# The place of two late steps, one on ScalarE and one on VectorE, in a kernel bound by TensorE

## The chip, the core and the metric

The kernel runs on one core of a Trainium2 chip. The metric is the device time of one execution in microseconds (us), as the median of several. The engines that matter are TensorE (PE in the profile; its weight loads are listed as PEld), VectorE (DVE), ScalarE (ACT) and SyncE (SP), which issues nearly all transfers. Each engine takes its instructions in the order in which the program lists them. They wait for one another through semaphores.

## What is computed

Eight batches of 256 tokens with 1024 features. Each batch goes through its own 1024 x 1024 matrix, chosen by an index. What comes out goes through one common 1024 x 1024 layer with a bias, and through a mixture of eight low-rank experts (rank 16) that a softmax router weighs. The input is added at the end.

```python
def cond(x, weight, adapter_ids):                  # per batch: y = x W[id]^T
    return jnp.einsum('bsi,boi->bso', x, weight[adapter_ids])

def ffn(x, base_W, base_b, router_W, router_b, A, B, expert_map):
    base_out = jnp.einsum('btd,od->bto', x, base_W) + base_b
    probs = jax.nn.softmax(jnp.einsum('btd,nd->btn', x, router_W) + router_b, axis=-1)   # 15 logits
    topk_p, topk_i = jax.lax.top_k(probs, E)                                             # E = 8
    onehot = (expert_map[topk_i][..., None] == jnp.arange(E)).astype(x.dtype)
    w = jnp.einsum('btk,btke->bte', topk_p, onehot)
    h = jnp.einsum('btd,erd->bter', x, A)                                                # R = 16
    return base_out + jnp.einsum('bter,eor->bto', h * w[..., None], B) * 2.0

out = x + ffn(cond(x, weight, ids), ...)
```

All of it is float32.

## The kernel before

The kernel has two stages. In both, PE, VectorE, ScalarE and SyncE take their instructions in the order in which the Python code writes them (`manual_schedule`), so a line that moves in the code moves in the queue of its engine.

**First stage, one batch after the other (the loop over b at L435).** The product of a batch with its matrix is done in the Strassen-Winograd manner: both sides are cut in four quadrants, and seven products of quadrants replace eight. Each of them is a `block` (L287): four float32 matmuls of 128 x 512, which the trace lists as eight. Three PSUM accumulators, pa, pb and pc, with two buffers each, collect the blocks. In batches 2 to 6 the blocks come in this order, with the quadrant sums S1 to S4 of the weights and T1 to T4 of x:

1. a11 b11 into pa; ScalarE copies pa to m0[:, 0] (L458).
2. a12 b21 into pb (`first_results`, L461); VectorE adds m0[:, 0] and transposes in squares of 32 (`flip`).
3. S1 T1 into pc; ScalarE copies pc to m1[:, 1] (L488).
4. S2 T2 added to pa; ScalarE copies pa to m0[:, 1] (L490).
5. S4 b22 added to pc (`by_s4`, L468); VectorE adds m0[:, 1] (L470) and transposes; then ScalarE moves all of m0, the first half of the result, to its place in y with sixteen copies of 32 partitions (`moves`, L308).
6. S3 b12 added to pa (`by_s3`, L474); VectorE adds m1[:, 1] (L476) and transposes.
7. `project` of the batch before (L129): PE multiplies y by the experts' A and the router's matrix together (143 columns, into ph, L136).
8. a22 T4 added to pa, which VectorE transposes into m1[:, 0].

The sixteen moves of the second half, m1, are left in `behind` for the next batch: four before the copy L458, twelve after it. VectorE works out the sums of the next batch's weights (L405 to L417) between its additions, and prepares the common layer's weights for the second stage (L325).

`project` also returns the steps of the routing: `logits` (with exp and the copy of h on ScalarE, L155 and L156), `softmax`, `top`, two `route_to` and `weigh` (L193), which multiplies h by the weights of the experts and transposes the product in squares of 32. After it stands a `turn` (L250): sixteen ScalarE copies of 32 x 64 elements (L255) that put the squares where they belong in hwT. In batches 2 to 7 the turn of the projection made one batch earlier is issued in `first_results`. In batches 2 to 6 that is after item 2. Batch 7 calls `first_results` later, after L490. Batch 0 and batch 1 have no turn to issue.

**Second stage, two groups of four batches (L679).** The common layer is multiplied in the Strassen-Winograd manner twice over. The outer seven products (the loop at L756) are each a `product` (L597) of seven inner blocks, now with 128 x 256 matmuls. Four of the seven outer products also add the experts' part (L588), from hwT. Between the inner blocks stand `gap(0)` to `gap(6)`. A gap runs the steps listed for it in `gaps`, which mostly append VectorE work to the queue `soon`; then `fill(2)` issues two entries of `soon`. After the last block the rest of `soon` is issued. The differences that the next product needs (L229) go to the head of `soon`, in gaps 0, 3 and 4.

The first outer product (n = 0, `here == 0`) also makes the first terms of the outer product with `first_terms`: for each of the four quarters (i, j) a pair of subtractions, y then t (L732). Quarters (0,0) and (0,1) enter in gap 1, (1,0) in gap 4, (1,1) in gap 6. Batch 6 was projected at the end of the first stage and only its `logits` were issued there; `steps_of` holds its five remaining routing steps, and they enter `soon` in gap 2 of this product. Its turn is issued after the next product, and batch 7 is projected there. ScalarE copies the first blocks of a product out of PSUM with the bias in the first outer product (L618); in the next ones VectorE does it, with an addition (L609).

Of the kernel before, what the change touches and what calls it, by code (L numbers as in the profile page):

```python
# [28 lines left out]
def kernel(  # L29
# [216 lines left out]
    def run(steps, n=None):  # L246
        for _ in range(len(steps) if n is None else min(n, len(steps))):
            steps.popleft()()

    def turn(b, hw):  # L250

        to = hwTs[b // GB][:, b % GB // 2, b % 2].rearrange("p (j a t) -> p j a t", j=NTT, a=4)
        return deque(
            (
                lambda a=a, r=r: nc.scalar.copy(  # L255
                    to[32 * r : 32 * r + 32, :, a, :],
                    hw[32 * a : 32 * a + 32, :, ts(r, 32)],
                )
            )
            for r in range(4)  # L260
            for a in range(4)
        )


    with ExitStack() as phase:
# [167 lines left out]
        waiting = None  # L433
        behind = deque()
        for b in range(B):  # L435
            last = b == B - 1

            b11, b12, b21, b22 = x[:, 0, 0], x[:, 1, 0], x[:, 0, 1], x[:, 1, 1]
            if not last:
                x, nq = load(b + 1)  # L440
            if b > 0:
                if not last:
                    third_sum(q)
                deque(prepare(b - 1))
                if last:
                    third_sum(q)
            prepare_load(b)
            if b == 1:
                nc.sync.dma_start(up[:, :2].rearrange("p h q o -> p (h q o)"), bT)

            pa = ps.tile([P, OH], F32, name="pa")
            pb = ps.tile([P, OH], F32, name="pb")
            pc = ps.tile([P, OH], F32, name="pc")

            m0, m1 = ms[:, 0], ms[:, 1]
            block(pa, q["a11"], b11, True)
            run(behind, 4)
            nc.scalar.copy(m0[:, 0], pa)  # L458
            run(behind)

            def first_results():  # L461
                block(pb, q["a12"], b21, True)
                nc.vector.tensor_add(m0[:, 0], pb, m0[:, 0])
                flip(m0[:, 0], m0[:, 0])
                if waiting:
                    run(turn(*waiting))

            def by_s4():  # L468
                block(pc, q["s4"], b22, False)
                nc.vector.tensor_add(m0[:, 1], pc, m0[:, 1])  # L470
                flip(m0[:, 1], m0[:, 1])
                run(moves(b, 0, m0))

            def by_s3():  # L474
                block(pa, q["a21"], b12, False)
                nc.vector.tensor_add(m1[:, 1], pa, m1[:, 1])  # L476
                flip(m1[:, 1], m1[:, 1])

            if not last:
                first_results()  # L480
            if b == 0:
                pd = ps.tile([P, OH], F32, name="pb")
                block(pd, q["a22"], t4, True)
                nc.scalar.copy(m1[:, 0], pd)
            if not last:
                nt1, nt2, nt4 = turns(x)
            block(pc, q["s1"], t1, True)
            nc.scalar.copy(m1[:, 1], pc)  # L488
            block(pa, q["s2"], t2, False)
            nc.scalar.copy(m0[:, 1], pa)  # L490
            if b == 0:
                by_s4()
                by_s3()
                nc.vector.tensor_add(m1[:, 0], pa, m1[:, 0])
                flip(m1[:, 0], m1[:, 0])
                first_sum(nq)
                second_sum(nq)
                fourth_sum(nq)
            elif not last:
                first_sum(nq)  # L500
                by_s4()
                if b == 1:

                    by_s3()
                    second_sum(nq)
                else:
                    second_sum(nq)
                    by_s3()
                fourth_sum(nq)
                ph = ps_h.tile([P, NTT, ER + N], F32, name="ph")  # L510
                steps, waiting = project(b - 1, ph)
                for step in steps[:3]:
                    step()
                block(pa, q["a22"], t4, False)
                flip(m1[:, 0], pa)
                for step in steps[3:]:
                    step()
            else:
                left[0] = load_left(lefts[0])
                terms = [step() for step in differences(yv[0][:, 0, 0])]  # L520
                first_results()
                by_s3()
                halves = prepare(b)
                next(halves)
                by_s4()
                deque(halves)
                block(pa, q["a22"], t4, False)
                flip(m1[:, 0], pa)
                left[1] = load_left(lefts[1])
                ph = ps_h.tile([P, NTT, ER + N], F32, name="ph")  # L530
                steps, waiting = project(b - 1, ph)
                steps.pop(0)()
            behind = moves(b, 1, m1)
            if not last:
                q, t1, t2, t4 = nq, nt1, nt2, nt4
            if b == 0:
                constants()
            if b == 1:
                nc.vector.tensor_sub(up[:, 2], up[:, 0], up[:, 1])
                nc.vector.tensor_sub(upd, up[:, :, 0], up[:, :, 1])  # L540
# [4 lines left out]
    with ExitStack() as phase:  # L545
# [21 lines left out]
        soon, later = deque(), deque()  # L567
        steps_of = steps
# [110 lines left out]
        for g in range(B // GB):  # L679
# [76 lines left out]
            for n, (right, base, into, done, *up_hw) in enumerate(seven):  # L756
                here = g * len(seven) + n
                gaps = {k: [] for k in range(7)}

                if n + 1 < len(seven):  # L760
                    follows = seven[n + 1][0]
                else:
                    follows = None if end else yv[g + 1][:, 0, 0]
                steps = [] if follows is None else differences(follows)
                nexts = []


                def advance(n, steps=steps, nexts=nexts):
                    def run():
                        soon.extendleft(  # L770
                            (lambda s=s: nexts.append(s())) for s in reversed(steps[n])
                        )

                    return run


                steps = [steps[:2], steps[2:3], steps[3:]]
                for k, m in ((0, 0), (3, 1), (4, 2)):
                    gaps[k].append(advance(m, steps))
                if here == 0:  # L780
                    gaps[2].append(lambda: soon.extend(steps_of))
                if n == 0:
                    gaps[1].append(lambda: first_terms((0, 0), (0, 1)))
                    gaps[4].append(lambda: first_terms((1, 0)))
                    gaps[6].append(lambda: first_terms((1, 1)))
                elif n in outer:
                    gaps[1].append(lambda n=n: soon.extend(outer[n]))
                if n in result_of:
                    for k, ij in enumerate([(0, 0), (1, 1), (0, 1), (1, 0)]):
                        gaps[k].append(lambda r=result_of[n] + ij: load_x(*r))  # L790
                if end and n == 6:

                    r = (1, 0, 1, 0)
                    gaps[5].append(
                        lambda: soon.append(lambda: add(u[:, 1, 0], u[:, 1, 0], xs[r]))
                    )
                if here == 0:
                    for k, count in enumerate((0, 1, 1, 4, 4, 4, 2)):
                        gaps[k].append(lambda count=count: run(behind, count))
                if here + 2 < len(lefts):  # L800

                    def fetch(m=here + 2):
                        left[m] = load_left(lefts[m])

                    gaps[5].append(fetch)
                product(
                    left.pop(here), terms, right, base, into, done, gaps, *up_hw,
                    *([None] * (2 - len(up_hw))), end and n == 6
                )
                terms = nexts  # L810
                if here == 1:
                    run(turn(*waiting))

                    ph = ps_e.tile([P, 2, S], F32, name="pe")
                    steps, waiting = project(B - 1, ph)
                    soon.extend(steps)
                elif here == 2:
                    run(turn(*waiting))
# [65 lines left out]
```

## Time and profile before

| | |
|---|---|
| median of 3 runs | 437.54 us (437.45 to 437.89) |
| the profiled execution | 437.13 us |
| its span, first to last instruction | 435.3 us |
| PE matmuls | 428.2 us busy (98%) |
| VectorE | 328.7 us (75%) |
| ScalarE | 166.7 us (38%) |
| sixteen copies of a turn (L255), 128 in all | 31.1 us, 243 ns each |
| moves (L308), 256 in all | 103.0 us, 402 ns each |
| granted TensorE clock, mean | 1.000 |
| first stage | up to 230.53 us |
| batches 3 to 6 | 28.32 us each |

The times in the trace count from the start of the span. The span is shorter than the time of the execution by 1.8 us, and the latter is what the median compares with. A line number in a row is that of the code that recorded the instruction, so blocks of the first stage all carry L290 and transposes L244; accumulators and tiles tell them apart. A matmul's end is modelled: rows of PE overlap a little, and the distance between starts says more than the durations.

### The profile page before, as it was taken

The page shows a single profiled execution, that of the slowest core. Times are in us where ns is not written, and L with a number is a line of the kernel's source. Part 1 is how long each engine was busy: PE and PEld are TensorE (multiplying, and loading weights), DVE is VectorE, ACT ScalarE, POOL GpSimd, SP SyncE. Part 2 cuts the span into 40 slices and gives each one's busy share as a digit, 9 for nine tenths or more (in the row PEclk, how much of TensorE's full clock was granted, in tenths as well). Part 3 has the DMA queues.
Part 4 walks back from the last instruction along what each step waited for, and adds up shares of the span by engine and source line. Part 5 has one row for each costly group of instructions (what it writes and reads, how often), then busy time and mean ns, then how long its engine had stood idle before and what let it go on. Part 6 is the DMA issues. An engine that isn't in the chain of part 4 may idle for free.

```text
span 435.3 us, 4931 instructions
## 1 busy us (share of the span) xinstructions
PE 428.2 (98%) x1642; PEld 293.3 (67%) x1642; DVE 328.7 (75%) x556; ACT 166.7 (38%) x458; POOL 0.7 (0%) x6
## 2 busy tenths in 40 slices
PE   8999998999999999999999999999999999999997
PEld 6344553644645446446459898888888888888886
DVE  0799999785887898988976866955597858745595
ACT  1029288665785676756928700300200200000200
POOL 0000000000000000000000000000000000000000
PEclk9999999999999999999999999999999999999999
DMA  7997987859587598791659555432968725912843
GB/s 276 416 347 256 369 332 287 304 174 353 177 302 273 223 318 304 270 333 78 209 230 372 226 179 234 159 132 78 373 227 275 274 77 201 392 62 63 300 152 139
DMA packets 32779, 106.05 MB, mean 244 GB/s; under 512 B 3058, under 2 KB 6898, under 8 KB 29554
## 3 DMA queue, kind: packets, MB, share of 16 engines
q1 hardware_dynamic: 32610, 105.21, 66.5%
q10 hardware_dynamic: 144, 0.52, 0.3%
q8 instruction: 13, 0.21, 0.2%
q14 instruction: 12, 0.10, 0.1%
HBM read 84.49 MB, written 21.23 MB: 243 GB/s over the span
## 4 chain that ended last, share of the span: by engine, by line
PE 70%; ACT 13%; DMA 7%; DVE 6%; SPq 2%; issue 2%; ACTq 0%; DVEq 0%
PE pa L579 20%; PE pa L290 14%; PE pc L579 10%; ACT y L308 7%; PE pc L290 6%; PE ph L136 5%; PE pb L579 5%; ACT hwT L255 4%; PE pc L588 3%; DMA wt<-in_wq_dram 2%; DMA late<-in_xr_dram 2%; DMA late<-in_ar_dram 2%; PE pb L588 2%; PE pa L588 1%; DVE wt L405 1%
## 5 line engine op out<-in xcount | busy, mean ns | idle before, releaser
L308 ACT COPY y<-late 32x256 f32<-32x256 f32 x256 | 103.0, 402 | 64.2 <-DVE late L244 61.3
L579 PE MATMUL pa<-tt,wt 128*128 128x256 f32 x324 | 78.2, 380 | 0.3 <-DVE q L609 0.3
L579 PEld LDWEIGHTS pa<-tt,wt 128*128 128x128 f32 x324 | 61.2, 190 | 9.6 <-DVE q L609 0.7
L290 PE MATMUL pa<-wt,x 128*128 128x512 f32 x128 | 57.5, 593 | 0.1
L290 PE MATMUL pa<-wt,tt 128*128 128x512 f32 x120 | 54.0, 593 | 0.0
L618 ACT ACTIVATE q<-pa,bb 128x256 f32<-128x256 f32 x12 | 5.0, 471 | 105.0 <-PE pa L579 104.0
L290 PEld LDWEIGHTS pa<-wt,x 128*128 128x128 f32 x128 | 24.2, 190 | 30.4 <-issue 30.2
L290 PEld LDWEIGHTS pa<-wt,tt 128*128 128x128 f32 x120 | 22.3, 190 | 26.2 <-issue 25.9
L255 ACT COPY hwT<-late 32x64 f32<-32x64 f32 x128 | 31.1, 243 | 7.6 <-DVE late L244 6.1
L290 PE MATMUL pc<-wt,x 128*128 128x512 f32 x64 | 29.4, 602 | 1.7 <-ACT late L488 1.3
L136 PEld LDWEIGHTS ph<-late,y 128*128 128x128 f32 x224 | 28.4, 189 | 3.3 <-issue 3.3
L290 PE MATMUL pb<-wt,x 128*128 128x512 f32 x64 | 29.0, 594 | 0.6 <-DMA wt<-in_wq_dram 0.6
L290 PE MATMUL pc<-wt,tt 128*128 128x512 f32 x64 | 28.8, 592 | 0.0
L136 PE MATMUL ph<-late,y 128*128 128x143 f32 x224 | 28.6, 284 | 0.0
L579 PE MATMUL pc<-tt,wt 128*128 128x256 f32 x112 | 27.8, 379 | 0.0
L290 PEld LDWEIGHTS pc<-wt,x 128*128 128x128 f32 x64 | 11.7, 190 | 19.0 <-issue 12.4
L405 DVE TENSOR_TENSOR wt<-wt 128x2048 f32<-128x2048 f32 (+1 forms) x9 | 18.4, 2046 | 7.9 <-PE pa L290 5.5
L579 PE MATMUL pc<-y,wt 128*128 128x256 f32 x96 | 24.0, 379 | 0.0
L579 PE MATMUL pb<-y,wt 128*128 128x256 f32 x96 | 24.0, 379 | 0.0
L579 PEld LDWEIGHTS pc<-tt,wt 128*128 128x128 f32 x112 | 21.3, 190 | 2.9
L290 PEld LDWEIGHTS pb<-wt,x 128*128 128x128 f32 x64 | 12.0, 190 | 16.3 <-issue 14.4
L290 PEld LDWEIGHTS pc<-wt,tt 128*128 128x128 f32 x64 | 12.1, 190 | 15.3 <-issue 14.6
(118 smaller groups left out, 548.9 us busy)
## 6 DMA issues: line engine op xcount, KB each, us to landing
wt<-in_wq_dram SPq DMA_DIRECT2D x28, 1024.0 KB, 5.5
wt<-left_raw SPq DMA_DIRECT2D x14, 1024.0 KB, 6.1
wt<-left_sum SPq DMA_DIRECT2D x14, 768.0 KB, 7.9
out_dram<-q SPq DMA_DIRECT2D x31, 256.0 KB, 2.3
x<-in_xq_dram SPq DMA_DIRECT2D x7, 1024.0 KB, 7.2
late<-in_xr_dram SPq DMA_DIRECT2D x20, 256.0 KB, 6.8
wt<-in_wq_dram SPq DMA_DIRECT2D x8, 512.0 KB, 7.3
spare<-in_bq_dram SPq DMA_DIRECT2D x4, 1024.0 KB, 5.4
```

What stands on the lines that cost most here:

```text
L136: nc.tensor.matmul(ph[:, j, : ER + N], lhsT=y[:, k // KH, th, k % KH // 2, bi, k % 2, ts(j, P)], rhs=ar_sb[:, k, :], start=(j == order[0] ...
L255: lambda a=a, r=r: nc.scalar.copy(to[32 * r : 32 * r + 32, :, a, :], hw[32 * a : 32 * a + 32, :, ts(r, 32)],)
L290: nc.tensor.matmul(acc, lhsT=right[:, k, :], rhs=left[:, k, :], start=(first and k == 0), stop=(k == KH - 1), skip_group_check=True,)
L308: lambda a=a, r=r: nc.scalar.copy(y[32 * r : 32 * r + 32, :, :, a, :], m[32 * a : 32 * a + 32, :, :, r, :])
L405: nc.vector.tensor_add(q["s1"][:, h], q["a21"][:, h], q["a22"][:, h])
L579: nc.tensor.matmul(acc[mi][:, mi, :], lhsT=left[:, 2 * k + mi, :], rhs=right[:, k, :], start=(first and k == 0 and (mi == 0 or acc[0] is n ...
L588: nc.tensor.matmul(acc[mi][:, mi, :], lhsT=up[:, ts(mi, P)], rhs=hw, start=False, stop=True, skip_group_check=True,)
L618: nc.scalar.activation(dst[:, mi], acc[mi][:, mi], AF.Identity, bias=bb[:, c : c + 1])
```

## The change

Two steps change their place. Nothing else does, and no instruction is added or removed.

- The turn leaves `first_results` and is issued after ScalarE's copy of S2 T2 (L490). In batch 7 that is where it stood. In the changed file all lines below L464 have numbers lower by two, up to the new place.
- The five routing steps of batch 6 enter `soon` in gap 6 of the first outer product, after the first terms of quarter (1,1), in place of gap 2.

```diff
@@ first_results @@
                 block(pb, q["a12"], b21, True)
                 nc.vector.tensor_add(m0[:, 0], pb, m0[:, 0])
                 flip(m0[:, 0], m0[:, 0])
-                if waiting:
-                    run(turn(*waiting))
@@ the loop over b @@
             nc.scalar.copy(m1[:, 1], pc)
             block(pa, q["s2"], t2, False)
             nc.scalar.copy(m0[:, 1], pa)
+            if waiting:
+                run(turn(*waiting))
             if b == 0:
                 by_s4()
                 by_s3()
@@ the loop over the outer products @@
-                if here == 0:
-                    gaps[2].append(lambda: soon.extend(steps_of))
                 if n == 0:
                     gaps[1].append(lambda: first_terms((0, 0), (0, 1)))
                     gaps[4].append(lambda: first_terms((1, 0)))
                     gaps[6].append(lambda: first_terms((1, 1)))
+                    if here == 0:
+                        gaps[6].append(lambda: soon.extend(steps_of))
```

## The prediction

> **What bounds the kernel now.** I read the page's busy line first: PE works in 98% of the span, so the most that any edit of order can win is PE's idle time and the short delays between its blocks. Next, the view of waits for PE, to see what it ever waits for (microseconds in total, times, longest):
>
> ```profile
> PE pb L427 <- POOL ident masks.py:199: 1.4, 1, 1.4
> PE pc L290 <- ACT late L488: 1.3, 1, 1.3
> PE pb L290 <- DMA wt<-in_wq_dram: 0.6, 1, 0.6
> PE pa L579 <- DVE q L609: 0.3, 1, 0.3
> ```
>
> The second and fourth row are the two places that the diff touches. The second understates its wait, because it counts only whole pauses; the timeline of PE shows the rest as starts that come late (start, duration, operation). First batch 2, then batch 4:
>
> ```profile
> 70.05 3.60 PE L290 MATMUL pa<-wt,tt 128*128 128x512 f32 x8
> 74.96 3.70 PE L290 MATMUL pc<-wt,x 128*128 128x512 f32 x8 [1.32 <-ACT late L488]
> 78.50 3.60 PE L290 MATMUL pa<-wt,x 128*128 128x512 f32 x8
> ...
> 124.47 3.60 PE L290 MATMUL pc<-wt,tt 128*128 128x512 f32 x8
> 127.91 3.60 PE L290 MATMUL pa<-wt,tt 128*128 128x512 f32 x8
> 131.61 3.70 PE L290 MATMUL pc<-wt,x 128*128 128x512 f32 x8
> ```
>
> An undisturbed block starts 127.91 - 124.47 = 3.44 us after the one before it; call it 3.43 (two in a row take 6.87 in the chain). The block by S4 (pc, from L469) starts 3.70 us after S2 T2 in batch 4, and 4.91 us after it in batch 2. It adds onto the PSUM that ScalarE's copy L488 must first have read. ScalarE's timeline in batch 4 says why that copy is late:
>
> ```profile
> 121.91 4.95 ACT L308 COPY y<-late 32x256 f32<-32x256 f32 x12
> 126.88 4.06 ACT L255 COPY hwT<-late 32x64 f32<-32x64 f32 x16
> 130.97 0.59 ACT L488 COPY late<-pc 128x512 f32<-128x512 f32 x1
> 131.54 0.59 ACT L490 COPY late<-pa 128x512 f32<-128x512 f32 x1
> 136.89 0.41 ACT L308 COPY y<-late 32x256 f32<-32x256 f32 x1 [4.76 <-DVE late L244]
> ```
>
> S1 T1 is done at 124.47 + 3.60 = 128.07, but L488 starts at 130.97, right behind the sixteen copies of L255, ends at 131.56, and PE starts at 131.61. After L490 ScalarE sits idle for 4.76 us.
>
> **Part 1, the sixteen copies behind L490.** They exist in batches 2 to 7; in batch 7 they stand behind L490 already, so five batches change. Nothing is added, and the step issues no DMA; it moves past two ScalarE copies and no other queue. Without it L488 starts when both the twelve moves and S1 T1 are done: in batch 4 at 128.1, ending 128.7, while S4 wants it at 127.91 + 3.43 = 131.34. In batch 2 the moves end at 70.21 and S1 T1 at 66.61 + 3.60 = 70.21, so L488 ends at 70.8, before 73.48. The wait goes.
>
> The gain is the distance from S2 T2 to S3 (pa, L475), less two blocks: batch 2: 78.50 - 70.05 - 6.87 = 1.58. Batches 3 to 6 (S2 T2 at 99.59, 127.91, 156.23, 184.55; S3 at 106.82, 135.14, 163.46, 191.79): 7.23, 7.23, 7.23, 7.24 less 6.87, 0.36 each, 1.45 together. Sum 3.03 us.
>
> What hides the copies in their new place is that idle 4.76 us. L490 ends at about 132.1; 4.06 us of copies and a gap bring 136.2. The moves behind them wait for VectorE's transpose of S4's result. S4 would now end at 131.34 + 3.60 = 134.94, the addition starts 0.1 later, the transpose 0.73 after that and lasts 0.71: 136.5. So 0.3 us of cover is left. If it were gone, the moves would be late by the excess, then exp (L155), for which VectorE already waits 0.46 us per batch, and next the transpose of pa, which has 0.88 us of idle before it; PE comes only after those. No reader of hwT comes before the second stage.
>
> VectorE must follow PE: in batch 2 the first sum starts at 74.72 on VectorE's own backlog and the next operation could start at about 76.9; S4's addition would be ready at 73.48 + 3.60 + 0.1 = 77.2. In batch 6 its idle time there is 1.12 us, and 0.36 of it is used. Nothing new becomes late.
>
> **Part 2, the weighing behind the first terms.** VectorE, in the first product of the second stage (start, duration; the last line is PE's timeline):
>
> ```profile
> 235.72 0.18 DVE L160 TENSOR_REDUCE late<-late 128x2 f32<-128x30 f32 x1
> ...
> 237.70 0.69 DVE L609 TENSOR_TENSOR u<-pb,u 128x512 f32<-128x512 f32 x1 [1.39 <-PE pb L579]
> ...
> 245.28 0.68 DVE L229 TENSOR_TENSOR tt<-t 128x512 f32<-128x512 f32 x1
> 246.07 0.69 DVE L229 TENSOR_TENSOR tt<-t,tt 128x512 f32<-128x512 f32 x1
> 246.68 0.68 DVE L609 TENSOR_TENSOR q<-pa,u 128x512 f32<-128x512 f32 x1
> ```
> ```profile
> 247.42 1.99 PE L579 MATMUL pa<-tt,wt 128*128 128x256 f32 x8 [0.32 <-DVE q L609]
> ```
>
> The addition at 246.68 empties pa for product 1's S2 T2, and PE waits for its end (247.37). The weighing now starts at 235.72 and runs partly in holes where VectorE would wait for PE anyway (1.39 us are left of one). The change takes it out of those holes and puts all of it between the last first term and the two differences (L229), so in front of that addition. Only y and t of quarter (1,0) come forward.
>
> The new order on VectorE, in the times of before (start to start: 0.61 us where an operation doesn't need the one ahead, 0.71 where it does):
> - u from pb at 237.70 (PE sets it), the difference 238.31, y(1,0) 238.91, u from pa 239.52, t(1,0) 240.12.
> - u from pc waits for PE's block (239.16 + 1.89 + 0.1): 241.15; y(1,1) 241.76; t(1,1) 242.47; end 243.08.
> - Softmax, three instructions (235.72 to 236.33 and the wait for its result): 0.63. Top, two maxima, two replacements, a difference (172.75 to 173.38 in batch 5, and 0.22 for the result): 0.85. Routing, weighing and transpose (L186 at 175.09 to the next operation at 177.08): 1.99. Sum 3.47: 246.55.
> - Two differences (245.28 to 246.68): 1.40, so the addition starts at 247.95, not at 246.68.
>
> That is 1.27 us later; I take 1.2 for the softer of these gaps. PE's S2 T2 starts as much later, and nothing behind it can catch up, as PE has no slack of its own. Bounds: at best the existing delay goes (from 242.61 to the b21 block at 249.25 is 6.64 us, against 28 records of 0.216 = 6.05: 0.59 gained); at worst nothing is won by the earlier y and t and the softmax, top and routing (0.63 + 0.85 + 1.0) all come on top: 2.5 lost. I take 1.2, as all its rows are of the same instructions. ScalarE's copies of batch 6 (243.54 now) start near 246.5; behind them ScalarE idles 18.33 us, and project's logits for batch 7 come later.
>
> **Sum.** -3.03 + 1.2 = -1.8 us. The profiled execution took 437.13 us around a span of 435.3, 0.41 below the median of 437.54; from that median: 435.7 us, 0.4% faster.
>
> **The rivals.**
> - *Part 2 costs nothing* (14%): if the weighing's small instructions overlap better than the rows in batch 5, or PE's start there is set by something else. The chain of waits names a transfer (late from the residual) ahead of the 246.68 addition, which speaks for it; but that addition starts 0.61 after the difference before it, the pace of no wait. Then -3.03: 434.5.
> - *Part 1 recovers only one of its two sorts of wait* (9%). Batch 1 has no sixteen copies and still loses 48.97 - 41.96 - 6.87 = 0.14, which speaks for a floor; but there the moves end at 44.76, behind S1 T1. If batch 2's 1.58 or the others' 1.45 stays: 437.2 to 437.3, no change.
> - *Slower: loads take the place of ScalarE* (7%). With PE ahead, the sums of the next batch's weights could wait for their transfers, and PE for the sums. The place is batch 2, where transfers are busy 1.01 of the time from 72 to 76 us. Its last three weight loads start between 66.8 and 70.2 and land 5.0, 6.5 and 8.0 us later; the second sum would now be wanted near 78.5 and its load is there near 75.5. It decides once landings are 3 us later than that; then part 1's gain is gone and part 2's price stays: 437.54 + 1.2 = 438.7. Against it: after 12.43 us PE waits for no transfer.
> - *PE's clock steps down after the longer pause in product 1* (4%). The pause grows from 0.5 to about 1.7 us. In batch 2 a pause of 1.32 us left the granted clock at 1.00 in the windows around it. The price, if it came, from the warm-up at the start: 26 records in 4.99 us, against 0.1225 each for the larger ones of L136 (3.92 us for 32): 1.8 us, so 437.5, no change. The Trainium skill, "TensorE: Matmul & The Clock Gate" (section "HAM oscillation — how this bites in real kernels") puts the gaps that drop the clock at more than about 3.4 us; by that rule neither pause does, and this trace agrees for 1.32 us.
>
> **How the numbers follow.** My forecast has 66%: 435.7, for itself 435.2 to 436.3. The range 434.3 to 437.0 also holds the case without part 2's cost and most sizes of it between the bounds, and leaves 20% outside. Faster by over 0.2% (0.88 us, about what a measurement here can tell from no change): 66 + 14 = 0.80. Same: 9 + 4 = 0.13. Slower: 0.07.
>
> **What would show it.** Right: no PE wait on L488's successor (L486 after), batches 2 to 6 at 27.96 us from one S3 to the next, as batch 7 has now (202.57 to 230.53), and PE reaching the second stage at 227.5 in place of 230.53; then a PE wait on VectorE's L609 in product 1 of about 1.5 us where 0.3 stood. Wrong: a second stage that starts later than 228.5, or product 1 as quick as before.

## The result and the profile after

The changed kernel takes 435.71 us (median of 6 runs, 435.38 to 436.07), against 437.50 us (6 runs, 437.21 to 437.89): 1.8 us less, a ratio of 0.9958 with a 95% interval of 0.9946 to 0.9971. The profiled execution took 435.38 us with a span of 433.6.

The waits of PE after the change (microseconds in total, times, longest):

```profile
PE pa L579 <- DVE q L609: 1.6, 1, 1.6
PE pb L427 <- POOL ident masks.py:199: 1.4, 1, 1.4
PE pb L290 <- DMA wt<-in_wq_dram: 0.4, 1, 0.4
PE pa L290 <- DMA wt<-in_wq_dram: 0.3, 1, 0.3
```

The wait for ScalarE's copy of pc is gone. The wait for VectorE in the second stage has grown from 0.3 to 1.6 us and is now the longest. PE's timeline shows the first in batches 2 and 4 (start, duration, operation):

```profile
70.13 3.60 PE L290 MATMUL pa<-wt,tt 128*128 128x512 f32 x8
73.56 3.60 PE L290 MATMUL pc<-wt,x 128*128 128x512 f32 x8
76.99 3.60 PE L290 MATMUL pa<-wt,x 128*128 128x512 f32 x8
...
126.03 3.60 PE L290 MATMUL pa<-wt,tt 128*128 128x512 f32 x8
129.47 3.60 PE L290 MATMUL pc<-wt,x 128*128 128x512 f32 x8
132.90 3.60 PE L290 MATMUL pa<-wt,x 128*128 128x512 f32 x8
```

S2 T2, S4 and S3 now follow each other at 3.43 to 3.44 us in both batches, where S4 had come 4.91 and 3.70 us after S2 T2. ScalarE in batch 4:

```profile
120.03 4.95 ACT L308 COPY y<-late 32x256 f32<-32x256 f32 x12
126.29 0.59 ACT L486 COPY late<-pc 128x512 f32<-128x512 f32 x1 [1.30 <-PE pc L290]
129.67 0.59 ACT L488 COPY late<-pa 128x512 f32<-128x512 f32 x1 [2.79 <-PE pa L290]
130.28 4.06 ACT L255 COPY hwT<-late 32x64 f32<-32x64 f32 x16
134.64 5.37 ACT L308 COPY y<-late 32x256 f32<-32x256 f32 x13 [0.30 <-DVE late L244]
```

The copy of pc (now L486) waits for PE, not PE for it. The sixteen copies fill ScalarE's idle time, of which 4.76 us has become 0.30, here and in each of batches 2 to 6: they fit, just.

The other side of the account, VectorE around the end of the first outer product and, last, PE in product 1 (the outer product after it):

```profile
234.72 0.69 DVE L609 TENSOR_TENSOR u<-pb,u 128x512 f32<-128x512 f32 x1 [1.90 <-PE pb L579]
...
238.18 0.69 DVE L609 TENSOR_TENSOR u<-pc,u 128x512 f32<-128x512 f32 x1 [0.36 <-PE pc L579]
...
240.11 0.18 DVE L160 TENSOR_REDUCE late<-late 128x2 f32<-128x30 f32 x1
...
243.56 0.65 DVE L229 TENSOR_TENSOR tt<-t 128x512 f32<-128x512 f32 x1
244.32 0.69 DVE L229 TENSOR_TENSOR tt<-t,tt 128x512 f32<-128x512 f32 x1
244.93 0.68 DVE L609 TENSOR_TENSOR q<-pa,u 128x512 f32<-128x512 f32 x1
```
```profile
245.66 1.99 PE L579 MATMUL pa<-tt,wt 128*128 128x256 f32 x8 [1.55 <-DVE q L609]
```

VectorE waits 1.90 us where it waited 1.39, and 0.36 us where it did not wait. From 240.11 to 243.56 it then does the whole weighing, while PE works towards a block that needs the addition at 244.93. Counted from the start of the second stage (230.53 before, 227.55 now), that addition starts at 17.38, where it started at 16.15.

### The profile page after: what moved, and what is told of

The parts are those of the page before. It is cut to its first block, busy times and chain, and to the rows that moved or that the text cites. A ratio compares the mean times of both kernels' runs of the same rounds, so it can differ in the third digit from the quotient of the medians.

```text
span 433.6 us, 4931 instructions
## 1 busy us (share of the span) xinstructions
PE 426.8 (98%) x1642; PEld 293.4 (68%) x1642; DVE 328.9 (76%) x556; ACT 166.9 (39%) x458; POOL 0.7 (0%) x6
## 4 chain that ended last, share of the span: by engine, by line
PE 95%; DMA 2%; DVE 2%; SPq 1%; issue 0%; DVEq 0%
PE pa L290 24%; PE pa L579 21%; PE pc L290 13%; PE pc L579 11%; PE pb L290 7%; PE ph L136 6%; PE pb L579 6%; PE pc L588 3%; DMA wt<-in_wq_dram 2%; PE pb L588 2%; PE pa L588 1%; PE pe L136 1%; PE pe L579 1%; SPq L359 0%; DMA ids_sb<-in_ids_dram 0%
## 5 line engine op out<-in xcount | busy, mean ns | idle before, releaser
L290 PEld LDWEIGHTS pa<-wt,x 128*128 128x128 f32 x128 | 24.2, 190 | 31.1 <-issue 30.2
L290 PEld LDWEIGHTS pc<-wt,tt 128*128 128x128 f32 x64 | 12.1, 190 | 15.3 <-issue 14.6
```

The lines of the kernel that those rows point to most:

```text
L290: nc.tensor.matmul(acc, lhsT=right[:, k, :], rhs=left[:, k, :], start=(first and k == 0), stop=(k == KH - 1), skip_group_check=True,)
```

## The experiments

To take each part by itself, I use two distances on PE's timeline that leave out the start of the execution: A from S2 T2 of batch 2 to the first block of the second stage, and B from there to the block a12 b21 of product 1.

| kernel | A, us | B, us | A + B against before | median, us |
|---|---|---|---|---|
| before | 160.48 | 18.72 | | 437.5 |
| the change | 157.42 | 19.95 | -1.83 | 435.71 |
| first part alone | 157.42 | 18.72 | -3.06 | 434.78 |
| second part alone | 160.51 | 19.95 | +1.26 | 438.78 |
| first part, weighing in product 1 | 157.42 | 18.13 | -3.65 | 433.80 |
| copies between the two | 158.41 | 18.73 | -2.06 | 435.31 |
| copies between, but batch 7 | 157.41 | 18.73 | -3.06 | 434.28 |
| copies behind the moves | 162.06 | 19.93 | +2.79 | 440.83 |

A and B come from one profiled execution each, a median from several, so the medians differ from A + B by some tenths. In the traces the start of an execution differs as much (see the last section). Nothing behind the two distances differs: in all eight traces the last matmuls start 182.45 to 182.47 us after the end of B.

**The first part alone.** Against the changed kernel:

```diff
+                if here == 0:
+                    gaps[2].append(lambda: soon.extend(steps_of))
...
-                    if here == 0:
-                        gaps[6].append(lambda: soon.extend(steps_of))
```

> The sixteen copies stand behind L490, the weighing of batch 6 stays in gap 2. My theory (two independent effects): the first stage ends 3.0 us earlier, the pause in product 1 stays at 0.3 us, and the time is 437.5 - 3.0 = 434.5 us. Rival (the two parts need each other, or part 2 was free and part 1 is worth 1.8 alone): 435.7 us.

434.78 us (5 runs, 434.15 to 435.18), a ratio of 0.9933 (0.9920 to 0.9947). A is that of the changed kernel to the hundredth, B is that of before. The first theory holds.

**The second part alone.** Against the changed kernel:

```diff
@@ first_results @@
+                if waiting:
+                    run(turn(*waiting))
@@ the loop over b, after the copy of pa @@
-            if waiting:
-                run(turn(*waiting))
```

> The sixteen copies stay in front of L488, the weighing of batch 6 goes to gap 6. My theory: the first stage still ends at 230.5 us, the pause in product 1 grows from 0.3 to 1.55 us, and the time is 437.5 + 1.2 = 438.7 us, a loss. Rival (the later weighing costs nothing by itself): 437.5 us.

438.78 us (6 runs), 1.0033 (1.0021 to 1.0045): a loss by itself. The three longest of PE's waits:

```profile
PE pa L579 <- DVE q L609: 1.6, 1, 1.6
PE pb L427 <- POOL ident masks.py:199: 1.4, 1, 1.4
PE pc L290 <- ACT late L488: 1.3, 1, 1.3
```

Both waits stand side by side, and the two parts' effects on A + B, -3.06 and +1.26, add up to the -1.83 of the change within 0.03 us. As far as these distances show, the parts don't touch each other.

**The weighing in product 1.** If PE's pause is the length of VectorE's queue ahead of one addition, the same work behind that addition should end the pause. Against the changed kernel:

```diff
+                if here == 1:
+                    gaps[2].append(lambda: soon.extend(steps_of))
...
-                    if here == 0:
-                        gaps[6].append(lambda: soon.extend(steps_of))
```

> As the changed kernel, but the five routing steps of batch 6 enter the queue of VectorE work in gap 2 of the second outer product, not in gap 6 of the first. My theory (PE's pause in product 1 is the length of what VectorE has queued ahead of the addition that empties pa): the pause goes altogether, 0.6 us more than before the change was there to win, and the holes of product 1 on VectorE (1.49, 1.30, 1.10 and 1.24 us of waiting in the trace of before) take the 3.5 us; 435.7 - 1.2 - 0.6 = 433.9 us. Rival (the weighing then delays the additions of product 1 and PE waits at S3 T3 or S4): 435 us or more, with a PE wait on L609 at another block.

433.80 us (5 runs, 433.17 to 434.53), 0.9913 (0.9899 to 0.9926): faster than both kernels. VectorE in product 1 of this kernel:

```profile
242.51 0.69 DVE L609 TENSOR_TENSOR q<-pa,u 128x512 f32<-128x512 f32 x1
245.10 0.69 DVE L609 TENSOR_TENSOR q<-pc,u 128x512 f32<-128x512 f32 x1 [1.90 <-PE pc L588]
245.71 0.17 DVE L160 TENSOR_REDUCE late<-late 128x2 f32<-128x30 f32 x1
...
249.42 0.69 DVE L609 TENSOR_TENSOR q<-pb,q 128x512 f32<-128x512 f32 x1 [0.55 <-PE pb L588]
```

The addition that empties pa starts 14.01 us into the second stage (242.51 - 228.50), 2.1 us earlier than before the change, and VectorE then waits for PE. PE waits for nobody in this product: S2 T2 starts at 244.90, 0.43 behind the last records of the block ahead of it at 244.47. The rival, a new wait at S3 T3 or S4, does not appear. B is 0.59 us below that of before, which is all of the delay that the prediction had counted as the most there was to win here.

**The copies between the two copies.** Which of the two did PE wait for? Against the first part alone:

```diff
             nc.scalar.copy(m1[:, 1], pc)
+            if waiting:
+                run(turn(*waiting))
             block(pa, q["s2"], t2, False)
             nc.scalar.copy(m0[:, 1], pa)
-            if waiting:
-                run(turn(*waiting))
```

> Part 1 in another place: the sixteen copies stand behind the copy of pc but in front of the copy of pa, the weighing stays in gap 2. My theory (PE waited for the copy of pc alone): the copy of pa then ends near 75.5 us in batch 2 and about 133.4 in batch 4 in the times of before, 1.4 us ahead of S3, so the time is that of the first part alone, 434.5 us, and the moves start no later. Rival (the copy of pa matters to PE or to VectorE's addition as well): part of the 3.0 us is given back, 435 to 437 us.

435.31 us (5 runs, 435.23 to 435.67), 0.9953 (0.9939 to 0.9966). The expectation missed. The timeline of PE in batch 7 holds all of the loss:

```profile
209.97 3.60 PE L290 MATMUL pb<-wt,x 128*128 128x512 f32 x8
214.29 3.70 PE L290 MATMUL pa<-wt,x 128*128 128x512 f32 x8 [0.72 <-ACT late L490]
217.83 3.60 PE L290 MATMUL pc<-wt,x 128*128 128x512 f32 x8
```

Batches 2 to 6 run without a gap, as my theory said, but I had forgotten batch 7. There PE goes from a11 b11 straight to S1 T1, so the twelve moves end later against PE, the copies reach past the end of a12 b21, and S3, which comes before S4 in this batch, waits for the copy of pa. From 209.97 to 217.83 it is 7.86 us in place of 6.87, the 0.99 by which A is longer.

**The same, but batch 7 as before.** Against the first part alone:

```diff
             nc.scalar.copy(m1[:, 1], pc)
+            if waiting and not last:
+                run(turn(*waiting))
...
             nc.scalar.copy(m0[:, 1], pa)
-            if waiting:
+            if waiting and last:
                 run(turn(*waiting))
```

> The sixteen copies between the copy of pc and the copy of pa in batches 2 to 6; in batch 7 behind both, as before the change; the weighing in gap 2. My theory (the run with the copies between the two in all batches lost 0.72 us plus the late start behind it in batch 7 alone, where S3 comes one block later but the twelve moves end only at 211.8 us): the wait of PE on L490 goes and the time is that of the first part alone, 434.8 us within 0.5. Rival (the late copy of pa costs something in every batch): 435.3 us as with the copies between the two everywhere.

434.28 us (5 runs, 434.00 to 434.63), 0.9923 (0.9909 to 0.9936), and A is 157.41: the loss was batch 7's alone. (A and B are those of the first part alone to 0.01 us; the two profiled executions differ by 0.78 us, and that lies ahead of S2 T2 of batch 2.) In batches 2 to 6 it is the copy of pc that PE waited for, and nothing else.

**The copies behind the moves.** The prediction said that 0.3 us of cover was left, and what would be late if it were gone. Here it is gone by 4 us. Against the first part alone:

```diff
@@ by_s4 @@
                 run(moves(b, 0, m0))
+                if waiting and not last:
+                    run(turn(*waiting))
@@ the loop over b, after the copy of pa @@
-            if waiting:
+            if waiting and last:
                 run(turn(*waiting))
```

> Part 1 with its cover taken away: in batches 2 to 6 the sixteen copies stand behind the sixteen moves of m0, directly in front of exp (L155); in batch 7 behind L490 as before the change; the weighing in gap 2. Both theories expect exp 4.1 us later and VectorE waiting for it some 4.5 us in place of 0.46. My theory (what the prediction said of the lost cover: VectorE's waits and the transpose of pa take it, and PE comes only after those, since VectorE works a batch ahead of PE with its sums): PE waits nowhere new and the time is that of the first part alone, 434.8 us within 0.5. Rival (exp is on the path of PE): each of five batches is longer, by up to 3.2 us (4.06 less the 0.88 of idle time), 436 to 450 us.

440.83 us (5 runs, 440.15 to 441.10), 1.0072 (1.0058 to 1.0086): slower than before the change. The expectation missed again, and the rival's range holds the time, though not by its account of a loss in each of five batches. Some of PE's waits:

```profile
PE pa L290 <- ACT late L458: 1.9, 1, 1.9
...
PE pa L290 <- DVE late L476: 1.1, 1, 1.1
PE pa L581 <- ACT u L620: 0.9, 1, 0.9
```

And the starts of the moves of m0 on ScalarE, batches 2 to 6:

```profile
78.85 6.61 ACT L308 COPY y<-late 32x256 f32<-32x256 f32 x16 [4.39 <-DVE late L244]
...
106.81 6.61 ACT L308 COPY y<-late 32x256 f32<-32x256 f32 x16 [4.39 <-DVE late L244]
...
134.76 6.62 ACT L308 COPY y<-late 32x256 f32<-32x256 f32 x16 [4.39 <-DVE late L244]
...
165.00 6.61 ACT L308 COPY y<-late 32x256 f32<-32x256 f32 x16 [6.67 <-DVE late L244]
...
195.23 6.61 ACT L308 COPY y<-late 32x256 f32<-32x256 f32 x16 [8.92 <-DVE late L244]
```

Up to 134.76 they are 27.96 and 27.95 us apart, PE's own pace: in batches 2 to 4 the 4.5 us for which VectorE waits for exp is swallowed whole. From then on they are 30.2 us apart. In batches 5 and 6 VectorE prepares four blocks of the common layer in place of three. The sum fits: in batches 3 and 4 VectorE had 21.85 us of its own work before the change, and with 4.54 of waiting that is less than PE's 27.96; in batches 5 and 6 it had 24.97, and with a wait of up to 4.78 that is more. No run has three blocks in batches 5 and 6, so the fourth block as the cause is argued from this sum, not shown. VectorE falls behind by 2.3 us per batch; late additions make ScalarE late. PE first waits in batch 6 (0.22 us at S4 for ScalarE's copy of pc, then 1.10 at a22 T4 for the addition of L476), then in batch 7 and in the first product of the second stage.

## Why the prediction was right

Its size came out because both effects did.

- *Part 1, -3.03 us.* A is 3.06 shorter. The place (the copy of pc, by the two experiments on where the copies stand), the two sorts of late start and the five batches are as written: with the change every one of the batches 2 to 6 runs at PE's pace. Their S3 start at 76.99, 104.95, 132.90, 160.85 and 188.81, 27.95 to 27.96 us apart. So the rival by which only one of the two sorts of wait is won back is out. Batch 1, which has no turn, keeps its 0.14 (42.03 to 49.04 now).
- *The cover of 0.3 us.* ScalarE's idle time ahead of the moves is 0.30 in all five batches of the profile after. What the prediction said of its loss was right in order (exp, VectorE, PE last) and had no size; I then took VectorE's slack for enough, and the last experiment shows that it is enough in batches 2 to 4 and not in 5 and 6. The change itself does not draw on it.
- *Part 2, +1.2 us.* B is 1.23 longer. The rows gave 1.27, rounded down for soft gaps; from its first instruction to the first difference the weighing takes 3.45 us (240.11 to 243.56), for 3.47 in the sum.
- *Loads in the place of ScalarE.* The waits of PE for transfers stay at the first batch, and from 20 to 231 us VectorE waits for none, before or after.
- *The clock.* PE's pause in product 1 is 1.55 us as its timeline flags it, and the granted clock of the whole span is 1.0. The rule that the prediction named there, of the Trainium skill, "TensorE: Matmul & The Clock Gate" (section "HAM oscillation — how this bites in real kernels"; gaps of more than about 3.4 us), is not contradicted, and no run here has a pause of PE that long: the longest is 1.93 us, with the copies behind the moves.
- *Part 2 costs nothing.* The chain of waits had named a transfer ahead of the addition. The weighing in product 1 decides. There the four transfers are issued 4.62 us into the second stage and later (233.12 to 235.3, from 228.50; 4.60 and later before) and take 10.0 us or more to land, so none is there before 14.6. The addition starts at 14.01, 2.1 us earlier than before, so it needs none of them: it was VectorE's queue, not the transfer.

## What to carry to other kernels

On an engine that takes its work in order, look for what stands in front of a PSUM copy that TensorE waits for, and move it into the next idle time of that engine; look at every iteration that has another order (batch 7 here), for the gain of the common ones hides its loss. A step with no near deadline belongs behind the operation that TensorE needs, not merely later: moved to the end of the product it cost 1.2 us, moved past the next deadline it gained 0.6. Cover is used up per iteration, so compare the work and waits of an engine with the pace in the busiest iterations: 4 us of extra waiting cost nothing in three batches and 6 us in all by the end.

## What was not expected of the hardware

The same 26 warm-up records at the start (L427) took from 4.64 us (the changed kernel) to 5.89 us (the copies between the two), though nothing ahead of them differs. But their length is not what the end of the execution sees. In all eight traces PE waits for a weight transfer for the last time in the middle of a12 b21 of the first batch, and goes on at 12.43 us (before) to 13.51 us (the first part alone). S2 T2 of batch 2 stands 57.61 to 57.64 us behind that point in every trace: at 70.05 us before, at 70.13 with the change, at 70.20 with the longest warm-up and at 71.14 with the first part alone. So one execution's span carries up to a microsecond that comes with the first loads and has nothing to do with a change of this size; why they land at different times is not shown. Distances between two points inside the trace are the sharper measure: A is 157.41 to 157.42 in four executions of four kernels.
